# A four-layer graph kernel: layer norm's squares and result moved to ScalarE, biases as products of ones, hub sums by halving additions, and slack for some steps

## The chip, the cores and the metric

The kernel runs on one core of a Trainium2 chip. The metric is the time of one execution in microseconds of the device. A core has five engines, each with its own queue that it works through in order: PE (TensorE: matrix products and transposes), DVE (VectorE), ACT (ScalarE), POOL (GpSimd, which here issues the gathers and scatters by index) and SP (SyncE, which issues plain DMAs). They wait for each other only through semaphores.

## What is computed

The inputs are `x` (16 graphs of 1024 nodes with 64 features), a dense 0/1 adjacency matrix of 1024x1024 for each graph, a node mask and the weights of four layers. Each layer is a residual step, `x = layernorm(x + layer(x, adj))`:

```python
def _layernorm(x, axis=-1, eps=1e-5):
    m = jnp.mean(x, axis=axis, keepdims=True)
    v = jnp.var(x, axis=axis, keepdims=True)
    return (x - m) / jnp.sqrt(v + eps)
```

- Layers 0 and 3 take a weighted sum of three quantiles (0.25, 0.5, 0.75) over the values of each node's neighbours, per feature, after some neighbours have been removed by a rule on their rank (dilation). Then `h = relu((x + agg) @ W1 + b1)`, `y = (h @ W2 + b2) * mask`.
- Layer 1 is `adj @ (x @ weight) + bias`.
- Layer 2 is attention, `gelu((softmax(m1 m2^T) + adj) @ x @ GCN_W)`.

## The kernel before

The path that runs is `listed_path` (line 784). For each graph, `graph` (L964) makes lists of neighbours: `neighbours` (L994) finds the removed ones, `both_ways` and `order` rank the nodes by degree, and `lists` (L1102) turns all into indices and weights. The 128 nodes of highest degree are the hubs. Their long lists are cut into chunks of 32 slots, `CH`; two blocks of `HC` = 59 columns of chunks hold them. The other nodes form seven tiles of 128 nodes with 22 to 8 slots (`TILE_CAPS`).

A quantile layer is done 32 times (16 graphs, layers 0 and 3; the order is in `layers`, L1262, where layer 3 of a graph comes two graphs after its layer 0). For each one:

- `fetch_stream` (L1287) has POOL gather one row of features for each slot: 60 gathers for the hubs (`hrows`, a ring of eight groups of two) and 89 for the other tiles (`rows`). Between them it puts the nine scatters (`sums`) of the layer before.
- `turn_stream` (L1323) transposes the hub rows on PE (`turned`) into columns, which ACT copies out (`cols`). A group of four must be turned before POOL may go on in the ring. At the end it transposes the sums `tot`.
- `sort_stream` (L1377) sorts on DVE: the hubs' columns (`long_lists`, L1412), then the tiles (`rows`). Inside `long_lists`, `summed` (L1465) multiplies the sorted values by weights `hw` and adds them up into `tot`.
- `pick_stream` (L1391) scales the sorted `rows` by weights on ACT and adds them on PE (`picked`); ACT copies the result to `agg`, which POOL scatters into `sums`.
- `middle_stream` (L1639) reads `sums` back and does `last_step` (L1519): two small matrix products, bias, mask, residual and `layernorm` (L942). After layer 0 it goes on with `spread_layer` (L1561, layer 1) and `attention_layer` (L1572, layer 2), each with a layer norm at its end. That is 64 layer norms in all, each on a tile of 128 partitions with 8 x 64 values (`[P, NT, C]`).

All these are Python generators of steps. `give_out` (L211) merges them at build time into one order for each engine. It keeps a clock for each engine with estimated costs (`Queue.times`, L183), and gives out, again and again, the step with the earliest time `max(engine free, inputs ready + slack)`. `.after(n)` sets a step's slack to n ns: the step is ranked as if its inputs came that much later, so that steps of other streams go in front. The hardware then runs each engine's order as it stands. An instruction that waits holds all behind it on its engine. All steps are issued at line 180, so groups are told apart by their tiles.

Of the kernel before, what the change touches and what calls it, by code (L numbers as in the profile page):

```python
# [8 lines left out]
F32 = mybir.dt.float32  # L9
# [6 lines left out]
AF = mybir.ActivationFunctionType  # L16
ALU = mybir.AluOpType
AX = mybir.AxisListType
# [16 lines left out]
HC = 59  # L35
# [5 lines left out]
CH = 32  # L41
# [221 lines left out]
EPS = 1e-5  # L263
# [520 lines left out]
def listed_path(ctx: ExitStack, tc: tile.TileContext, x, adj, nodemask,  # L784
                l0_w1, l0_b1, l0_w2, l0_b2, l1_w, l1_b,
                l2_w1, l2_w2, l2_g, l3_w1, l3_b1, l3_w2, l3_b2, out, fp):
    nc = tc.nc
    B, N, C = x.shape
    H = l0_w1.shape[1]
    P = 128  # L790
# [90 lines left out]
    V.memset(w_scale[:, 0:1], 0.25)  # L881
    V.memset(w_scale[:, 1:2], 0.5)


    def load(ap, shape, name):
        t = const.tile(shape, F32, name=name)
        nc.sync.dma_start(t, ap)
        return t

    def rows(ap, name):  # L890
        t = const.tile([P, C], F32, name=name)
        nc.sync.dma_start(t, ap.rearrange("(o c) -> o c", o=1).to_broadcast([P, C]))
        return t

    ends = []
    for k, (w1, b1, w2, b2) in enumerate(((l0_w1, l0_b1, l0_w2, l0_b2), (l3_w1, l3_b1, l3_w2, l3_b2))):
        ends.append((load(w1, [C, H], f"w1_{k}"), load(b1.rearrange("(h o) -> h o", o=1), [H, 1], f"b1_{k}"),
                     load(w2, [H, C], f"w2_{k}"), rows(b2, f"b2_{k}")))
    l1w = load(l1_w, [C, C], "l1w")
    l1b = rows(l1_b, "l1b")  # L900

    l2g = const.tile([C + 1, C + 1], F32, name="l2g")
    V.memset(l2g, 0.0)
# [35 lines left out]
    def one(shape):  # L939
        return psm.tile(shape, F32, name="one", bufs=2)  # L940

    def layernorm(z, sq, y):  # L942
        s = small["t"].tile([P, NT], F32, name="ln_s")
        yield V.tensor_reduce(s, z, AX.X, ALU.add)
        mean = small["t"].tile([P, NT], F32, name="ln_mean")
        yield V.tensor_scalar(mean, s, 1.0 / C, None, ALU.mult)
        yield V.tensor_tensor(z, z, mean.unsqueeze(2).to_broadcast([P, NT, C]), ALU.subtract)
        yield V.tensor_mul(sq, z, z)
        v = small["t"].tile([P, NT], F32, name="ln_v")
        yield V.tensor_reduce(v, sq, AX.X, ALU.add)  # L950
        yield V.tensor_scalar(v, v, 1.0 / C, EPS, ALU.mult, ALU.add)
        r = small["t"].tile([P, NT], F32, name="ln_r")
        yield A.activation(r, v, AF.Sqrt)

        q = small["t"].tile([P, NT], F32, name="ln_q")
        yield V.reciprocal(q, r)
        yield V.tensor_mul(q, q, v)
        yield V.tensor_add(q, q, r)
        yield V.tensor_scalar(q, q, 0.5, None, ALU.mult)
        yield V.reciprocal(q, q)  # L960
        yield V.tensor_mul(y, z, q.unsqueeze(2).to_broadcast([P, NT, C]))
        return y

    def graph(b, k):  # L964
# [29 lines left out]
    def neighbours(np, psn, b, k, near, nbt):  # L994
# [24 lines left out]


        mi = small["g"].tile([P, NT], I32, name="mi")
        yield V.tensor_scalar(mi, pm, 1.0, None, ALU.add)
        do = small["g"].tile([P, NT], F32, name="do")
        yield V.scalar_tensor_tensor(do, pm, 10.0, k.mask, ALU.is_gt, ALU.mult)
        yield V.tensor_scalar(mi, mi, 1, None, ALU.logical_shift_right)
# [17 lines left out]
        for t in range(NT):  # L1043
            mine = slice(t * P, (t + 1) * P)
            v = np.tile([P, N], F16, name="v", tag="h", bufs=3)
            yield A.activation(v, pq.rearrange("p h n -> p (h n)"), AF.Abs, bias=mid[:, t:t + 1])
            gone = np.tile([P, N], F16, name="gone", tag="h", bufs=3)
            yield V.tensor_scalar(gone, v, off[:, t:t + 1], None, ALU.is_equal)
            if t + 1 < NT:
                pq = yield from counted(t + 1)  # L1050

            for h in range(NH):
                pn = psn.tile([P, HALF], F32, name="one")
                yield T.matmul(pn, neg16, gone[:, h * HALF:(h + 1) * HALF], start=True, stop=False)
                for j in range(HALF // P):
                    yield T.matmul(pn[:, j * P:(j + 1) * P], nbt[:, h * (HALF // P) + j, mine], ident16,
                                   start=False, stop=(j == HALF // P - 1))
                yield A.copy(near[:, t, h * HALF:(h + 1) * HALF], pn)
            pg = psn.tile([P, NT, P], F16, name="pg", tag="one")
            for j in range(NT):  # L1060
                yield T.transpose(pg[:, j, :], gone[:, j * P:(j + 1) * P], ident16)
            yield A.copy(nbt[:, :, mine], pg)
# [39 lines left out]
    def lists(lp, psl, b, near, perm, deg, k):  # L1102
# [46 lines left out]
        for q in range(GC):  # L1149
            yield T.matmul(pi, quarter[:, q], named.rearrange("s h (g q) -> s q h g", q=GC)[:, q],  # L1150
                           start=(q == 0), stop=(q == GC - 1))
        yield V.tensor_copy(k.hidx, pi)
        events.add(("hidx", b))


        for g in range(1, NT):
            pk = psl.tile([P, NH, HALF], F32, name="two")
            for h in range(NH):
                cols = slice(h * HALF, (h + 1) * HALF)
                yield T.matmul(pk[:, h], ones16[0:1, :], key_row[:, cols], start=True, stop=False)  # L1160
                for t in range(NT):
                    yield T.matmul(pk[:, h], perm[:, t, g * P:(g + 1) * P], near[:, t, cols],
                             start=False, stop=(t == NT - 1))
            cap = TILE_CAPS[g - 1]
            top = lp.tile([P, MOST + 2], F32, name="top", bufs=2)
            keys = pk.rearrange("p h n -> p (h n)")
            for r in range((cap + 7) // 8):
                yield V.max(out=top[:, 8 * r:8 * r + 8], in_=keys)
                if 8 * r + 8 < cap:
                    rest = lp.tile([P, N], F32, name="rest", bufs=2)  # L1170
                    yield V.match_replace(out=rest, in_to_replace=top[:, 8 * r:8 * r + 8], in_values=keys,
                                    imm_value=-4096.0)
                    keys = rest
            yield V.tensor_scalar(k.idx[:, g - 1, :cap], top[:, :cap], 0.0, None, ALU.max)
# [148 lines left out]
    def turn_stream():  # L1323
        for n, (l, b) in enumerate(layers):
# [3 lines left out]
            for g in range(0, NG, 4):  # L1328
                pt = psh.tile([P, 4 * P], F32, name="turned")
                for i in range(g, min(g + 4, NG)):  # L1330
                    yield Wait("h", n, i)
                    e = min(P, (2 * HC - i * GC) * CH)
                    yield T.transpose(pt[:, (i - g) * P:(i - g) * P + e], k.hrows[i][:e].rearrange("p h c -> p (h c)"),
                                      ident[:e, :e]).after(3000)
                events.add(("turned", n, g // 4))
                first, end = g * GC, min((g + 4) * GC, 2 * HC)
                for i in range(2):
# [74 lines left out]
    def long_lists(n, k):  # L1412
# [52 lines left out]
        def summed(block, spans):  # L1465

            yield Wait("hw", n, block)
            for c0, c1 in spans:
                assert len(set(side[c0:c1])) == 1
                v = bufs[side[c0]][block][:, :, c0 % HC:c0 % HC + c1 - c0]  # L1470
                yield V.tensor_tensor(v, v, k.hw[block][:, :, c0 % HC:c0 % HC + c1 - c0], ALU.mult)
            more = None
            for c0, first, lists, k0, chunks, by_list in HUB_RUNS:
                if c0 // HC == block:
                    v = bufs[side[c0]][block][:, :, c0 % HC:c0 % HC + lists * chunks]
                    v = v.rearrange("p s (l k) -> p l k s" if by_list else "p s (k l) -> p l k s", k=chunks)
                    if k0:
                        more = qp.tile([P, lists], F32, name="more")
                    yield V.tensor_reduce(more if k0 else k.tot[:, first:first + lists], v, AX.XY, ALU.add)
                    if k0:  # L1480
                        yield V.tensor_add(k.tot[:, first:first + lists], k.tot[:, first:first + lists], more)
            events.add(("block", n, block))

        yield from first(0)
# [34 lines left out]
    def last_step(n, l, b, k):  # L1519
# [6 lines left out]
        yield D.dma_start(ag, by_part(k.sums)).after(8000)  # L1526
        yield V.tensor_add(ag, ag, xn).after(5000)
        py = one([P, NT, C])
        for h in range(NH):
            ts = range(h * (HALF // P), (h + 1) * (HALF // P))  # L1530
            pt = one([C, HALF])
# [7 lines left out]
            yield A.activation(ht, ph, AF.Relu, bias=b1)  # L1539
            for t in ts:  # L1540
                c0 = t % (HALF // P) * P
                yield T.matmul(py[:, t, :], ht[:, c0:c0 + P], w2, start=True, stop=True)
        z = features("z")
        yield V.tensor_tensor(z, py, b2.unsqueeze(1).to_broadcast([P, NT, C]), ALU.add)
        yield V.tensor_mul(z, z, k.mask.unsqueeze(2).to_broadcast([P, NT, C]))
        yield V.tensor_add(z, z, xn)
        return (yield from layernorm(z, ag, features("y")))

    def by_adj(k, xn):
# [11 lines left out]
    def spread_layer(xn, k, y):  # L1561

        at_x = yield from by_adj(k, xn)
        po = one([P, NT, C])
        for t in range(NT):
            yield T.matmul(po[:, t, :], at_x[:, t * P:(t + 1) * P], l1w, start=True, stop=True)
        z = features("z")
        yield V.tensor_tensor(z, po, l1b.unsqueeze(1).to_broadcast([P, NT, C]), ALU.add)
        yield V.tensor_add(z, z, xn)
        return (yield from layernorm(z, features("ag"), y))  # L1570

    def attention_layer(xn, k, y):  # L1572
# [141 lines left out]
```

## Time and profile before

| | |
|---|---|
| Median of 3 runs | 8266.02 us (8259.21 to 8276.33) |
| The profiled execution, its own time | 8298.99 us |
| Its span in the trace | 8297.2 us |
| Mean granted TensorE clock in it | 0.738 |
| POOL: gathers and scatters | 5056 instructions, between 0.9 and 1.5 us each as a rule |
| First gather | 192.67 us after the span's start |
| ACT table loads | 50, 1283 ns each |

The span runs from the first to the last instruction. "Busy" time of an engine leaves out the time in which it issues or waits. The list of waits gives, for each pair of a waiting instruction and what released it, the total time, the number of times and the longest. A group of instructions is written as out<-in by the names of the tiles.

### The profile page before, as it was taken

Reading aid. Unit: us, or ns where it says so; the run is one execution under the profiler, and the core shown is the slowest. Engines: PE = TensorE matmul, PEld = TensorE weight load, DVE = VectorE, ACT = ScalarE, POOL = GpSimd, SP = SyncE. Lnnn points to the kernel's source line nnn. Section 1 sums busy time; section 2 is a strip of 40 time slices with the busy share of each in tenths; the row PEclk is TensorE's granted clock in tenths of the full one; section 3 lists DMA queues with packets and bytes.
Section 4 is the critical chain, followed back from the end, with each engine's and each line's share of the span. In section 5 each row is a group of like instructions: output and inputs, shape, how many; then the busy total and the mean of one; then the engine's idle time right before and its main releaser. Section 6 shows DMA issues by size and latency. Waiting matters only on the chain. (4 is left out here: it accounts for less than half of the span.)

```text
span 8297.2 us, 81388 instructions
## 1 busy us (share of the span) xinstructions
PE 5196.2 (63%) x24851; PEld 2751.4 (33%) x24851; DVE 7057.9 (85%) x14774; ACT 2329.8 (28%) x5554; POOL 5693.1 (69%) x5087
## 2 busy tenths in 40 slices
PE   6568777758475675856658575665856668272541
PEld 4244333333332333433233333323333233131221
DVE  2779798789898898988889898898988889979795
ACT  3324334142322324132242313324232232121121
POOL 0734677667776776767767676777767777777774
PEclk8778887878686776877778686777867678565565
DMA  1331423232323222232322324222332222232221
GB/s 48 72 72 50 99 44 97 46 77 65 73 50 89 52 55 69 62 81 52 63 63 66 73 50 94 52 51 69 72 71 52 65 61 65 33 68 33 58 42 22
DMA packets 762008, 513.78 MB, mean 62 GB/s; under 512 B 459098, under 2 KB 600538, under 8 KB 761306
## 3 DMA queue, kind: packets, MB, share of 16 engines
q1 hardware_dynamic: 457434, 261.99, 13.0%
q0 software_dynamic: 161792, 163.90, 11.6%
q10 hardware_dynamic: 142336, 82.59, 3.4%
q8 instruction: 201, 3.29, 0.2%
q14 instruction: 245, 2.01, 0.1%
HBM read 408.73 MB, written 103.55 MB: 62 GB/s over the span
## 5 line engine op out<-in xcount | busy, mean ns | idle before, releaser
L180 POOL DMA_INDIRECT rows<-table,idx x2848 | 3264.6, 1146 | 867.9 <-issue 841.1
L180 POOL DMA_INDIRECT hrows<-table,hidx x1920 | 2096.4, 1092 | 928.8 <-issue 443.1
L180 DVE TENSOR_TENSOR spare<-cols 128x528 f32<-128x528 f32 (+11 forms) x1632 | 1057.1, 674 | 71.4 <-ACT cols L180 47.7
L180 DVE TENSOR_TENSOR cols<-spare 128x528 f32<-128x528 f32 (+11 forms) x1664 | 1074.8, 680 | 15.8
L180 PE MATMUL picked<-rows,ident 128*128 128x64 f32 (+2 forms) x2496 | 646.1, 366 | 347.6 <-ACT rows L180 346.6
L180 PE MATMUL turned<-ident,hrows 128*128 128x128 f32 x960 | 343.1, 379 | 673.6 <-DMA hrows<-table,hidx 636.3
L180 POOL DMA_INDIRECT sums<-agg,node x224 | 260.2, 1162 | 665.2 <-DMA sums<-agg,node 195.3
L180 ACT ACTIVATE rows<-rows,wt 128x64 f32<-128x64 f32 x2272 | 612.5, 340 | 191.2 <-DVE rows L180 188.5
L180 PEld LDWEIGHTS picked<-rows,ident 128*128 128x128 f32 x2496 | 479.7, 244 | 543.1 <-ACT rows L180 446.3
L180 PE MATMUL pi<-hot,numbers 128*32 128x236 f16 x4096 | 549.4, 284 | 76.0 <-DVE hot L180 74.4
L180 DVE TENSOR_TENSOR spare<-rows 128x64 f32<-128x64 f32 (+8 forms) x1056 | 539.0, 541 | 58.1 <-DMA sums<-hagg,hnode 21.7
L180 PE MATMUL two<-near,perm 128*128 128x512 f16 x1792 | 544.6, 459 | 0.0
L180 PEld LDWEIGHTS <-numbers 128*32 128x32 f16 x4096 | 397.0, 103 | 331.8 <-issue 275.7
L180 ACT COPY cols<-turned 128x512 f32<-128x512 f32 (+3 forms) x288 | 148.5, 528 | 1253.8 <-PE turned L180 1252.9
L180 PE MATMUL two<-run,nbt 128*128 128x512 f16 (+3 forms) x1536 | 408.9, 438 | 142.4 <-ACT v L180 142.4
L180 PEld LDWEIGHTS turned<-ident,hrows 128*128 128x128 f32 x960 | 163.4, 175 | 926.5 <-issue 591.9
L180 PEld LDWEIGHTS <-nbt 128*128 128x128 f16 x3584 | 303.6, 113 | 491.4 <-issue 416.9
L180 DVE TENSOR_TENSOR rows<-spare 128x512 f32<-128x512 f32 (+9 forms) x896 | 462.5, 538 | 0.8
L180 PE MATMUL turned<-ident,tot 128*64 128x128 f32 x32 | 11.7, 365 | 609.4 <-DVE tot L180 609.4
L180 DVE TENSOR_TENSOR spare<-cols,spare 128x472 f32<-128x472 f32 (+2 forms) x704 | 379.2, 539 | 15.6
L180 PE MATMUL one<-xt,wt 64*128 64x512 f32 x512 | 369.8, 851 | 22.0 <-DVE top L180 22.0
L180 DVE TENSOR_TENSOR rows<-rows,spare 128x64 f32<-128x64 f32 (+4 forms) x1120 | 363.2, 329 | 17.6
(232 smaller groups left out, 10079.9 us busy)
## 6 DMA issues: line engine op xcount, KB each, us to landing
at<-adjt SPq DMA_DIRECT2D x512, 256.0 KB
a<-in_adj_dram SPq DMA_DIRECT2D x128, 512.0 KB
adjt<-at ACTq DMA_DIRECT2D x128, 512.0 KB
rows<-table,idx POOLq DMA_INDIRECT x2848
hrows<-table,hidx POOLq DMA_INDIRECT x1920
hw<-hwt SPq DMA_DIRECT2D x64, 472.0 KB
hwt<-ho ACTq DMA_DIRECT2D x64, 236.0 KB
ag<-sums SPq DMA_DIRECT2D x32, 256.0 KB
```

The source lines that it names most:

```text
L180: return Step(lambda: f(*args, **kw), self.engine, cost, late, reads, writes, "dma" in name)
```

## The change

- In `layernorm`, the subtraction of the mean, the product z*z and its sum over features leave DVE. ACT makes for each of the eight tiles of nodes a `Square` of z with the negative mean as bias, which also accumulates the sum. The result `y = z*q - mean*q` is made by eight ACT instructions with scale and bias in place of one DVE product; DVE gets a small product `mean*q`.
- In `last_step` and `spread_layer` the bias is no longer added on DVE. A matrix product of a row of ones with the bias row starts the accumulation in PSUM, and the others add to it. The bias is loaded as one row and not copied to 128 partitions. The mask is applied by eight scaled ACT copies out of PSUM; the residual is added on DVE.
- In `summed`, the weighted values go into one buffer, and the 32 slots are added by halves: 16, 8, 4, 2, 1. Then each run of lists needs one small operation on its chunks.
- Some steps get slack: `ln_v` 2000, the first `reciprocal` 1000, `mi` 3000, `gone` 2000, `hidx` 3000, the first `max` of each tile 1500, `z + xn` in `last_step` 6000 and `z` in `spread_layer` 3000; the transposes of the hub rows go from 3000 to 6000.

```diff
@@ layernorm
-        yield V.tensor_scalar(mean, s, 1.0 / C, None, ALU.mult)
-        yield V.tensor_tensor(z, z, mean.unsqueeze(2).to_broadcast([P, NT, C]), ALU.subtract)
-        yield V.tensor_mul(sq, z, z)
+        yield V.tensor_scalar(mean, s, -1.0 / C, None, ALU.mult)
         v = small["t"].tile([P, NT], F32, name="ln_v")
-        yield V.tensor_reduce(v, sq, AX.X, ALU.add)
-        yield V.tensor_scalar(v, v, 1.0 / C, EPS, ALU.mult, ALU.add)
+        for t in range(NT):
+            yield A.activation(sq[:, t], z[:, t], AF.Square, bias=mean[:, t:t + 1], accum_out=v[:, t:t + 1])
+        yield V.tensor_scalar(v, v, 1.0 / C, EPS, ALU.mult, ALU.add).after(2000)
...
-        yield V.reciprocal(q, r)
+        yield V.reciprocal(q, r).after(1000)
...
-        yield V.tensor_mul(y, z, q.unsqueeze(2).to_broadcast([P, NT, C]))
+        yield V.tensor_mul(mean, mean, q)
+        for t in range(NT):
+            yield A.activation(y[:, t], z[:, t], AF.Identity, scale=q[:, t:t + 1], bias=mean[:, t:t + 1])
@@ neighbours
-        yield V.tensor_scalar(mi, pm, 1.0, None, ALU.add)
+        yield V.tensor_scalar(mi, pm, 1.0, None, ALU.add).after(3000)
...
-            yield V.tensor_scalar(gone, v, off[:, t:t + 1], None, ALU.is_equal)
+            yield V.tensor_scalar(gone, v, off[:, t:t + 1], None, ALU.is_equal).after(2000)
@@ lists
-        yield V.tensor_copy(k.hidx, pi)
+        yield V.tensor_copy(k.hidx, pi).after(3000)
...
-                yield V.max(out=top[:, 8 * r:8 * r + 8], in_=keys)
+                yield V.max(out=top[:, 8 * r:8 * r + 8], in_=keys).after(0 if r else 1500)
@@ turn_stream
-                                      ident[:e, :e]).after(3000)
+                                      ident[:e, :e]).after(6000)
@@ summed
+            w = bufs[side[spans[0][0]]][block]
             for c0, c1 in spans:
                 assert len(set(side[c0:c1])) == 1
-                v = bufs[side[c0]][block][:, :, c0 % HC:c0 % HC + c1 - c0]
-                yield V.tensor_tensor(v, v, k.hw[block][:, :, c0 % HC:c0 % HC + c1 - c0], ALU.mult)
-            more = None
+                cols = slice(c0 % HC, c0 % HC + c1 - c0)
+                yield V.tensor_tensor(w[:, :, cols], bufs[side[c0]][block][:, :, cols], k.hw[block][:, :, cols], ALU.mult)
+            half = CH // 2
+            while half:
+                yield V.tensor_add(w[:, :half], w[:, :half], w[:, half:2 * half])
+                half //= 2
             for c0, first, lists, k0, chunks, by_list in HUB_RUNS:
                 if c0 // HC == block:
-                    v = bufs[side[c0]][block][:, :, c0 % HC:c0 % HC + lists * chunks]
-                    v = v.rearrange("p s (l k) -> p l k s" if by_list else "p s (k l) -> p l k s", k=chunks)
+                    v = w[:, 0, c0 % HC:c0 % HC + lists * chunks]
+                    v = v.rearrange("p (l k) -> p l k" if by_list else "p (k l) -> p l k", k=chunks)
+                    mine = k.tot[:, first:first + lists]
                     if k0:
-                        more = qp.tile([P, lists], F32, name="more")
-                    yield V.tensor_reduce(more if k0 else k.tot[:, first:first + lists], v, AX.XY, ALU.add)
-                    if k0:
-                        yield V.tensor_add(k.tot[:, first:first + lists], k.tot[:, first:first + lists], more)
+                        yield V.tensor_add(mine, mine, v[:, :, 0])
+                    elif chunks == 1:
+                        yield V.tensor_copy(mine, v[:, :, 0])
+                    elif chunks == 2:
+                        yield V.tensor_add(mine, v[:, :, 0], v[:, :, 1])
+                    else:
+                        yield V.tensor_reduce(mine, v, AX.X, ALU.add)
@@ last_step
         py = one([P, NT, C])
+        yield T.matmul(py, ones_row, b2.unsqueeze(1).to_broadcast([1, NT, C]), start=True, stop=False)
...
-                yield T.matmul(py[:, t, :], ht[:, c0:c0 + P], w2, start=True, stop=True)
+                yield T.matmul(py[:, t, :], ht[:, c0:c0 + P], w2, start=False, stop=(t == NT - 1))
         z = features("z")
-        yield V.tensor_tensor(z, py, b2.unsqueeze(1).to_broadcast([P, NT, C]), ALU.add)
-        yield V.tensor_mul(z, z, k.mask.unsqueeze(2).to_broadcast([P, NT, C]))
-        yield V.tensor_add(z, z, xn)
+        for t in range(NT):
+            yield A.activation(z[:, t], py[:, t], AF.Copy, scale=k.mask[:, t:t + 1])
+        yield V.tensor_add(z, z, xn).after(6000)
@@ spread_layer
         po = one([P, NT, C])
+        yield T.matmul(po, ones_row, l1b.unsqueeze(1).to_broadcast([1, NT, C]), start=True, stop=False)
         for t in range(NT):
-            yield T.matmul(po[:, t, :], at_x[:, t * P:(t + 1) * P], l1w, start=True, stop=True)
+            yield T.matmul(po[:, t, :], at_x[:, t * P:(t + 1) * P], l1w, start=False, stop=(t == NT - 1))
         z = features("z")
-        yield V.tensor_tensor(z, po, l1b.unsqueeze(1).to_broadcast([P, NT, C]), ALU.add)
-        yield V.tensor_add(z, z, xn)
+        yield V.tensor_tensor(z, po, xn, ALU.add).after(3000)
```

The rest of the diff makes the row of ones and loads the three biases as rows.

More of the change, by code (lines that the diff above doesn't have):

```diff
@@ L882, in listed_path @@
     V.memset(w_scale[:, 1:2], 0.5)
+    ones_row = const.tile([1, P], F32, name="ones_row")
+    V.memset(ones_row, 1.0)
     def load(ap, shape, name):
@@ L888, in load, with row @@
         return t
[L890 to L893, printed above, removed]
+    def row(ap, name):
+        return load(ap.rearrange("(o c) -> o c", o=1), [1, C], name)
     ends = []
@@ L897, in listed_path @@
         ends.append((load(w1, [C, H], f"w1_{k}"), load(b1.rearrange("(h o) -> h o", o=1), [H, 1], f"b1_{k}"),
-                     load(w2, [H, C], f"w2_{k}"), rows(b2, f"b2_{k}")))
+                     load(w2, [H, C], f"w2_{k}"), row(b2, f"b2_{k}")))
     l1w = load(l1_w, [C, C], "l1w")
-    l1b = rows(l1_b, "l1b")
+    l1b = row(l1_b, "l1b")
     l2g = const.tile([C + 1, C + 1], F32, name="l2g")
```

## The prediction

> **What bounds the kernel now.** I read the page first (busy shares, then the 40 slices), then the lists of POOL's and DVE's waits, then groups with their shapes, and last one stretch of the timeline.
>
> ```profile
> span 8297.2 us, 81388 instructions
> PE 5196.2 (63%) x24851; PEld 2751.4 (33%) x24851; DVE 7057.9 (85%) x14774; ACT 2329.8 (28%) x5554; POOL 5693.1 (69%) x5087
> POOL 0734677667776776767767676777767777777774
> L180 POOL DMA_INDIRECT rows<-table,idx x2848 | 3264.6, 1146 | 867.9 <-issue 841.1
> ```
>
> DVE leads with 85%, ACT has room. But POOL's 69% misleads: a gather takes 1.15 us, and then 0.30 us (868 us over 2848) pass in which it waits for nothing. A POOL that never waits still shows 7 tenths. What can be won there stands in the list of its waits (us in total, times, longest):
>
> ```profile
> POOL sums L180 <- DMA sums<-agg,node: 195.3, 109, 4.1
> POOL sums L180 <- ACT rows L180: 186.1, 34, 52.7
> POOL hrows L180 <- DVE hidx L180: 184.3, 1, 184.3
> POOL sums L180 <- ACT agg L180: 182.9, 19, 36.4
> POOL hrows L180 <- PE turned L180: 177.2, 99, 23.7
> ```
>
> The first is the scatters' own order and stays; the third is the start. ACT rows 186, ACT agg 183, PE turned 177 and the smaller ones (DVE rows, cols, spare, z, top and PE one: 89) make 635. Without them the span is 8297 - 635 = 7662, **POOL's floor**. In the steady part, 2000 to 7000 us, the same list gives 280: PE 112, ACT 109, DVE 59. DVE's own list:
>
> ```profile
> DVE gone L180 <- ACT v L180: 251.1, 105, 8.3
> DVE z L180 <- PE one L180: 227.5, 26, 18.2
> DVE top L180 <- PE two L180: 151.6, 57, 17.9
> DVE top L180 <- PE one L180: 56.4, 82, 2.2
> DVE hidx L180 <- PE pi L180: 53.2, 13, 6.5
> ```
>
> So two engines are near full. How one late engine holds the others shows at the end of one layer's hub work (start, duration, instruction, idle before it):
>
> ```profile
> 4096.16 1.23 DVE L180 TENSOR_REDUCE tot<-cols 128x20 f32<-128x640 f32 x1
> ...
> 4097.45 0.42 PE L180 MATMUL turned<-ident,tot 128*64 128x128 f32 x1 [37.73 <-DVE tot L180]
> ...
> 4098.97 1.45 POOL L180 DMA_INDIRECT hrows<-table,hidx  x1 [7.73 <-PE turned L180]
> ```
>
> DVE finished `tot` late; PE stood 37.7 us, and POOL, whose ring of hub rows was full, 7.7 us. DVE's instructions just ahead held a whole layer norm. This is why less DVE work should reach the end.
>
> **The change, part by part.** *Layer norm, 64 times.* Removed from DVE: `z<-z,ln_mean` 683 ns, `ag<-z` 682, `ln_v<-ag` 676, `y<-z,ln_q` 684, so 2.73 us; added: `mean*q`, like `ln_q<-ln_q,ln_v`, 0.16. Net 2.56 x 64 = 164 us. Added to ACT: 8 squares and 8 scalings of 128x64. The row for 128x64 with one column operand is `rows<-rows,wt`, 340 ns; an accumulated sum costs 220 to 241 more (the READ_ACCUMULATOR rows behind `near` and `v`). Squares: 8 x 0.57 = 4.6 us. Scalings have two column operands, which no row shows: at least the 214 of `agg<-picked` 128x64 without one, at most twice 340; nearest is 340, and I take that: 2.7. Together 7.3 x 64 = 467 us of ACT (bounds 400 to 640).
>
> *Biases and mask.* In `last_step` two DVE instructions go (692 + 683 ns, x32 = 44 us), and 8 scaled copies of 128x64 from PSUM come on ACT: 8 x 0.34 x 32 = 87 us. In `spread_layer` one of two goes: 0.68 x 16 = 11 us. PE gets 48 products of a row of ones, 512 columns wide; the nearest row is `one<-xt,wt` with 512 columns, 851 ns: 41 us, from nothing to that. They need no input of the layer and run ahead of the transposes, so PE's 37% idle time hides them; without that cover they cost the 41. The bias loads become smaller at the start; the start waits 184 us for the first lists, which hides that.
>
> *Hub sums, 32 times.* Removed, by shape: reductions of 2895, 632, 579, 415, 576, 794, 468 and 1232 ns and an addition of 165: 7.76 us. Added per block: additions of 944, 472, 236, 118 and 59 columns, by equal shapes 1150 + 650 + 404 + 281 + 214 = 2.70, twice; and eight small ones at 146 to 205 ns, 1.33 in all. 6.73 us, a gain of 1.03 x 32 = 33 us. But each halving waits for the one before, while independent instructions overlap: in the timeline the next starts some 0.08 us before the last ends. Ten links of 0.1 us eat 1.0 per layer. So this edit is worth 0 to 33; I take 16.
>
> DVE loses 164 + 44 + 11 + 16 = **235 us**.
>
> *Slack.* It moves a step to a later place among DVE's (or PE's) instructions; no instruction is added, and no DMA is among the moved ones. The steps it reaches on DVE wait 251 (`gone`) + 227 (`z`, whose sum now waits behind ACT's copies) + 152 (`top` from `two`) + 53 (`hidx`) + 27 (`mi`) + 15 (`ln_q`) = 726 us now, 422 of them in the steady part. The mean wait of `gone` is 2.4 us against a slack of 2; of `z` 8.7 against 6; of `hidx` 4.1 against 3. So I take half, 363. The wait of `z` for PE passes to ACT's copies: 227 us, behind which on ACT stand `v`, `cols` and `rows`; ACT's idle 72% covers it, and what it costs without that cover is rival (c). 122 of `top` and 103 of `gone` fall before 2000 us, where other work to put in front is scarce. New waits: `ln_v` now waits for eight squares on ACT, and behind it on DVE stand the sorts; cover is the slack of 2 us. At nothing to 4.6 us each it costs 0 to 294; I take 0.7, since ACT's `ln_r` held DVE only 15.3 us in 64. That is 45. So DVE's waits fall by 363 - 45, about 320.
>
> Doubling the transposes' slack to 6000 is two-sided: PE waits 636 us for `hrows` now, which should shrink; but the transposes free POOL's ring, eight groups or 22 us of gathers, and later ones can lengthen the 177.
>
> DVE's occupied time falls by 235 + 320 = 555. POOL can follow only as far as its 635, and what it wins is what counts. **Sum:** steady part: the waits released by DVE go (59); of PE's 112 two thirds (75), since the stretch above shows DVE behind them and the ring's slack speaks against all; of ACT's 109 half (54), as DVE comes sooner but ACT has more to do. 188. Outside it POOL waits for whole chains at the start; there I credit DVE's smaller work alone, 235 x 3297/8297 = 93. The tail is one serial chain: squares and scalings 7.3 + mask 2.7 for DVE's 2.56 + 1.37, so 6 longer. 188 + 93 - 6 = 275. The profiled execution takes 8299.0 by its own time (span 8297.2), the median of runs is 8266.0, 0.4% less. 8299 - 275 = 8024, by 0.996: **7992**, so 7990.
>
> One rule speaks against the change: the Trainium skill, ScalarE: Activation LUTs, section "Rules for kernel authors", wants multiply and add on VectorE, not ScalarE. The row agrees on the price: one 128x512 is 0.68 us on DVE, and 8 x 0.34 = 2.7 on ACT. Were the engine's own price what counts, layer norm and mask would add 554 - 208 = 346 us; but ACT is 28% busy and DVE 85%, so the page's rule does not decide here. The same page, section "What ACT_TABLE_LOAD costs", says that each pointer operand adds about 93 ns: an estimate from it for the scalings is 340 + 93 = 433 ns, which would make ACT's addition 515 instead of 467; no row shows it.
>
> **Rivals.**
> (a) *The slack gives nothing* (it does not do what it says): the waits move to the next step, as real lateness exceeds it. Then DVE gives 235 - 45 = 190, of which POOL follows about half, 95 to 130: 8135 to 8240, say 8170. For it: `gone`'s and `z`'s mean waits are above their slacks.
> (b) *DVE held nearly everything*: POOL's waits mostly go, 450 to 550 of 635: 7720 to 7820, say 7770. For it: the stretch above. Against: the scatters' waits at the start pass through ACT.
> (c) *Slower: ACT's queue.* Layer norm's 16 instructions stand in order on ACT, and wait for `ln_mean`, then for `q` on DVE (`ln_r` waits 247 us in 64 now, up to 36). Behind them are the scalings of `rows` and the copies of `agg`, for which POOL's scatters wait, and behind those all gathers. It decides from 275/64 = 4.3 us of extra POOL wait per layer norm. At 6 of its 7.3 us passed on: 384 - 275 = +109, 8375. For it: POOL's 369 us for ACT rows and agg. Against: ACT still ends near 36% busy (2330 + 554 of 8000), and only 109 of these lie in the steady part.
>
> **Chances.** Forecast, 7840 to 8130: 0.55. (a) 0.18. (b) 0.12, a little below it included. (c) 0.12. No change 0.03. The range leaves out (c), no change, and the outer part of (b), 0.05: 7750 to 8240. A measurement of this kernel tells about 0.2% from no change. Faster 0.85, same 0.03, slower 0.12.
>
> **What would show it.** DVE's busy time near 6820 us; ACT's near 2880 with squares near 340 ns and their accumulator reads near 220; `gone`, `z`, `top` and `hidx` with half their waits; POOL's waits for PE turned, ACT agg and ACT rows down from 546 to some 350. Wrong would be: POOL's waits for ACT grown; a gather that takes another time than 1.15 us (the floor moves: 0.1 us is 285 us over `rows`); new DVE waits for `ln_v` near 4 us; or PE turned grown by the ring.

## The result and the profile after

The kernel after takes 8255.0 us (median of 12 runs, 8217.05 to 8279.63); the kernel before on the same chip 8272.6 us (12 runs, 8258.16 to 8288.93). The ratio is 0.9974, with a 95% interval of 0.996 to 0.9988. So it is faster, clear of noise but only by a quarter of a percent: 17.6 us where some 275 were forecast, outside the range. The profiled execution has a span of 8258.9 us, 38 less than before's profiled one; half of that lies in the two executions picked, as the medians differ by 17.6 only. In two of the later batches, on two chips, every kernel took 13 to 17% longer, before 17%, with waits on PE, ACT and DVE that the profile puts to nothing in the program; the eight runs there are told as ratios alone, and six of those kernels were run again (labels ending in `_2`; "the first run" below is the one of these batches).

The page of after, its head, POOL's slices and the group of the gathers (busy, mean ns, idle time ahead):

```profile
span 8258.9 us, 83245 instructions
PE 5314.9 (64%) x24947; PEld 2777.2 (34%) x24947; DVE 6878.5 (83%) x14791; ACT 2726.7 (33%) x7346; POOL 5640.8 (68%) x5087
POOL 0635567657676776767777676777777777777774
L180 POOL DMA_INDIRECT rows<-table,idx x2848 | 3247.0, 1140 | 868.0 <-issue 840.3
```

DVE did lose work (7057.9 to 6878.5) and ACT gained it (2329.8 to 2726.7). POOL's slices, of 207 us each, have lost a tenth in the second, fifth, sixth, ninth and eleventh, and from the twelfth on in none: something is late in the first 2300 us that was not before. POOL's list of waits after:

```profile
POOL hrows L180 <- PE turned L180: 316.1, 110, 57.4
POOL hrows L180 <- DVE hidx L180: 180.3, 1, 180.3
POOL sums L180 <- DMA sums<-agg,node: 175.3, 99, 5.3
POOL sums L180 <- ACT rows L180: 150.2, 19, 45.7
POOL sums L180 <- ACT agg L180: 105.6, 5, 29.7
```

The waits for ACT fell from 369 to 256 us, but `PE turned` rose from 177 to 316. DVE's list:

```profile
DVE top L180 <- PE two L180: 161.9, 61, 6.7
DVE z L180 <- ACT z L180: 159.8, 27, 39.7
DVE deg L180 <- ACT near L180: 143.1, 12, 17.3
DVE gone L180 <- ACT v L180: 124.5, 77, 9.2
DVE top L180 <- PE one L180: 99.6, 80, 4.5
DVE ln_v L180 <- ACT ag L180: 66.1, 30, 3.8
...
DVE rs L180 <- PE one L180: 46.9, 26, 6.0
```

`gone` halved (251 to 125), `z` fell by 68, `hidx` from 53 to 7. In their place stand `top` (208 to 262 in its two rows), `ln_v`, and two that had hardly waited in before:

```profile
DVE deg L180 <- ACT near L180: 17.3, 1, 17.3
DVE rs L180 <- PE one L180: 1.9, 2, 1.7
```

All idle times of DVE over 0.1 us together went up, from 1069 to 1185 us.

**By stage.** The transposes of `tot`, one for each of the 32 quantile layers, cut the span into equal pieces of work (L0 to L31). Two layers make a pair, since the odd ones are shorter; the steady piece is L7 to L25, nine pairs. "POOL's own" is its gathers, the gaps of 0.3 us behind them and the scatters' own order; the rest of a pair are waits for other engines, with 1 to 3 us of gaps that the profile puts to nothing. Each figure comes from one execution, and the runs of after alone lie up to 63 us apart, so two or three us per pair tell nothing.

| us | L1 to L7 | one pair, L7 to L25 | POOL's own | POOL's waits | DVE busy / waits | L25 to L31 | after L31 |
|---|---|---|---|---|---|---|---|
| before | 1618.9 | 495.7 | 467.8 | 27.9 | 438.4 / 48.0 | 1322.1 | 160.4 |
| after | 1667.6 | 484.9 | 458.8 | 26.2 | 427.4 / 46.8 | 1325.8 | 168.8 |

Of the 38 us between the two spans, nine pairs bring 97; the layers 1 to 7 give 49 back, all from L25 on 12. And the pair's gain is not the one forecast: 9 of its 10.8 us are POOL's own time, not waits. About half of the 9 are shorter gathers and scatters (357.6 to 353.1 us busy per pair), the other half is the scatters' own order (18.4 to 13.7).

### The profile page after: what moved, and what is told of

Read it like the earlier page. It is cut to its first block, busy times and chain, and to the rows that moved or that the text cites. A ratio compares the mean times of both kernels' runs of the same rounds, so it can differ in the third digit from the quotient of the medians.

```text
span 8258.9 us, 83245 instructions
## 1 busy us (share of the span) xinstructions
PE 5314.9 (64%) x24947; PEld 2777.2 (34%) x24947; DVE 6878.5 (83%) x14791; ACT 2726.7 (33%) x7346; POOL 5640.8 (68%) x5087
## 3 DMA queue, kind: packets, MB, share of 16 engines
q1 hardware_dynamic: 457008, 261.89, 13.3%
## 5 line engine op out<-in xcount | busy, mean ns | idle before, releaser
L180 POOL DMA_INDIRECT hrows<-table,hidx x1920 | 2054.8, 1070 | 1069.3 <-issue 457.2
L180 PE MATMUL picked<-rows,ident 128*128 128x64 f32 (+2 forms) x2496 | 676.0, 388 | 399.8 <-ACT rows L180 398.9
L180 PEld LDWEIGHTS picked<-rows,ident 128*128 128x128 f32 x2496 | 500.8, 259 | 557.9 <-ACT rows L180 483.3
L180 PE MATMUL two<-run,nbt 128*128 128x512 f16 (+3 forms) x1536 | 426.4, 452 | 238.0 <-ACT v L180 238.0
L180 PE MATMUL pi<-hot,numbers 128*32 128x236 f16 x4096 | 521.1, 273 | 70.1 <-DVE hot L180 66.1
L180 PE MATMUL two<-near,perm 128*128 128x512 f16 x1792 | 507.0, 434 | 0.0
L180 DVE TENSOR_TENSOR spare<-spare 128x944 f32<-128x944 f32 (+11 forms) x672 | 451.2, 671 | 19.1
```

Source lines behind the costliest of these rows:

```text
L180: return Step(lambda: f(*args, **kw), self.engine, cost, late, reads, writes, "dma" in name)
```

## The experiments

The first theory was that POOL's own pace sets the steady time, so that DVE's saving has nothing to shorten there, and that the slacks only move waits about. The rivals were that ACT's longer layer norm takes the gain back, and that the doubled slack of the transposes does (where expectations use letters, P is the first theory, Q and R are these two rivals). All ratios are against before on the same chip.

| kernel | us | ratio (95%) | L1 to L7 | pair | POOL's own / waits | DVE busy / waits |
|---|---|---|---|---|---|---|
| no_slack | 8329.9 | 1.008 (1.0063 to 1.0098) | 1636.1 | 494.9 | 464.6 / 30.3 | 426.1 / 58.2 |
| slack_only | 8360.6 | 1.0109 (1.0094 to 1.0125) | 1637.1 | 498.3 | 464.6 / 33.7 | 439.0 / 49.9 |
| turned_3000 | 8272.1 | 0.9998 (0.9987 to 1.0009) | 1661.8 | 489.9 | 462.9 / 27.0 | 427.6 / 51.5 |
| ln_back_2 | 8327.8 | 1.0068 (1.0052 to 1.0085) | 1628.4 | 494.7 | 466.4 / 28.3 | 434.3 / 50.3 |
| deg_slack_2 | 8311.0 | 1.0035 (1.0023 to 1.0048) | 1676.1 | 490.1 | 467.9 / 22.2 | 425.1 / 54.6 |
| late_slack_2000_2 | 8214.9 | 0.9913 (0.9896 to 0.9929) | 1619.6 | 485.5 | 461.4 / 24.1 | 427.3 / 47.4 |
| pool_1480_2 | 8208.9 | 0.9916 (0.9902 to 0.9931) | 1634.7 | 482.6 | 468.1 / 14.5 | 427.2 / 44.7 |
| no_inside | 8094.4 | 0.9779 (0.9765 to 0.9793) | 1643.0 | 477.8 | 450.0 / 27.8 | 384.6 / 83.4 |
| half_hub_2 | 7894.3 | 0.9526 (0.9505 to 0.9547) | 1590.6 | 469.7 | 377.5 / 92.2 | 426.1 / 32.8 |
| half_both_2 | 7746.9 | 0.9348 (0.9329 to 0.9367) | 1542.5 | 467.5 | 372.2 / 95.3 | 384.6 / 72.9 |

After, no_slack, turned_3000, deg_slack_2, late_slack_2000_2 and pool_1480_2 hold the same instructions in six orders, and take from 8209 to 8330 us. So a difference of some tens of us between kernels with different instructions cannot be put to the instructions alone, the 17.6 us of the change included.

**no_slack**: the change's arithmetic without any new slack.

```diff
-        yield V.tensor_scalar(v, v, 1.0 / C, EPS, ALU.mult, ALU.add).after(2000)
+        yield V.tensor_scalar(v, v, 1.0 / C, EPS, ALU.mult, ALU.add)
...
-                                      ident[:e, :e]).after(6000)
+                                      ident[:e, :e]).after(3000)
```

> The changed kernel with every new slack taken back (the transposes of hub rows at 3000 again), its arithmetic kept. Theory P (in steady state POOL bounds and takes nearly the same time per pair of layers whatever DVE saves; what was gained there, some 105 us, is lost again at layers 2 and 5, where the new order lets POOL stand): the loss of 60 us at layers 2 and 5 goes, a pair of layers stays at 484 to 495 us, so 8140 to 8210 us. Rival Q (ACT's 400 us of new work and its new waits hold the copies behind them, and that eats the gain): ACT's work is the same, and DVE's waits come back, so 8250 to 8320. Rival R (the longer slack of the transposes lengthens POOL's ring wait, 177 to 316 us): the 140 us come back, near 8115.

8329.9 us, slower than before, though DVE's busy time per pair is 12 us lower. Its lists of POOL's and of DVE's waits have

```profile
POOL hrows L180 <- PE turned L180: 287.8, 101, 28.9
```

```profile
DVE gone L180 <- ACT v L180: 280.7, 97, 9.1
DVE z L180 <- ACT z L180: 244.5, 30, 32.9
```

DVE's saved time shows up again as DVE's waits (48.0 to 58.2 per pair), and POOL's did not shrink (30.3). So the change's arithmetic, which takes work from DVE, buys nothing in this order. The time is above what P (8140 to 8210) and Q (8250 to 8320) expected.

**slack_only**: before, with the same slacks on its own steps.

```diff
-            yield V.tensor_scalar(gone, v, off[:, t:t + 1], None, ALU.is_equal)
+            yield V.tensor_scalar(gone, v, off[:, t:t + 1], None, ALU.is_equal).after(2000)
```

> The kernel before with the slacks alone (on its own steps: z = py + b2 with 6000, the one in the spread layer with 3000, the rest as in the change, none on ln_v). P: the loss at the early layers comes without the arithmetic's gain; steady pairs at 485 to 495: 8270 to 8340 us. Q: DVE's waits go and ACT gets no work, so clearly faster, near 8150. R: POOL's ring waits grow as in the change, so slower by 100 or more, near 8370.

8360.6 us, slower too, above P's 8270 to 8340 and near R's 8370; the next run speaks against R. The slacks do not pay by themselves either. Arithmetic (+0.8%) and slacks (+1.1%) together give -0.26%: the effects do not add up. Each version is another order of all engines.

**turned_3000**: only the transposes' slack back to 3000.

> The changed kernel with the transposes of the hub rows at 3000 again, all else kept. R: POOL's waits for PE turned fall from 316 to some 180 us, time 8110 to 8150. P: the early loss stays, the ring matters little: within 25 us of the changed kernel. Q: no change of ACT's work: the same.

8272.1 us, 17 more than after (0.9998 against 0.9974): the doubled slack helps a little. The theory that it takes the gain away, which had 8110 to 8150 here, falls.

**ln_back**: the layer norm of before, all else as after.

```diff
-        for t in range(NT):
-            yield A.activation(sq[:, t], z[:, t], AF.Square, bias=mean[:, t:t + 1], accum_out=v[:, t:t + 1])
+        yield V.tensor_mul(sq, z, z)
...
+        yield V.tensor_reduce(v, sq, AX.X, ALU.add)
```

> The changed kernel with the layer norm of before (on DVE, without its slacks); biases, mask, hub sums and the other slacks as in the change. DVE gets 164 us back, ACT loses 453 us. Q (ACT's layer norm holds the copies and scalings behind it): faster than the change, 8150 to 8220. P (DVE's work is not what bounds): within 30 us of 8255. If DVE's work mattered as the prediction had it: 8255 + 100, 8340 or more.

> The change without layer norm's move to ACT, as in ln_back, on another chip. Q (ACT's new work eats the gain): 8150 to 8220. P (neither DVE's nor ACT's share of work is what bounds): within 30 us of 8255. DVE's work matters as predicted: 8340 or more.

The two runs differ in sign. The first gives 0.9834 (0.979 to 0.9878). The second gives 8327.8 us, 73 more than after: outside P's 30 us, and just under the 8340 of a DVE whose work counts. The theory of ACT's queue, which had 8150 to 8220, is not borne out by it. How much of the 73 us is layer norm's work is not shown, as orders of the same instructions differ by more.

**no_inside**: does DVE set the pace? Of the hubs' sort, four of the five passes inside the chunks are left out.

```diff
-            for j in (16, 8, 4, 2, 1):
+            for j in (1,):
```

> The changed kernel with four of the five passes of the hub sort inside chunks left out (only the pass of distance 1 is made), so that the hub values are not fully sorted; this takes some 730 us from DVE (per layer 8 instructions less for each of four widths: 2 x (988+705+804+372) x 4 ns) and nothing from POOL, PE or ACT. P: POOL's gathers remain, and a pair of layers cannot fall below some 467 us: 7850 to 8000 us. A theory that DVE still bounds: near 8255 - 730 x 0.85, about 7630. Q: ACT's and PE's waits for DVE shrink too, 7700 to 7800.

DVE's busy time falls by 42.8 us per pair, the pair by 7.1; DVE's waits rise from 46.8 to 83.4. What the pair did gain is POOL's own time (458.8 to 450.0), because the same gathers got shorter:

```profile
L180 POOL DMA_INDIRECT rows<-table,idx x2848 | 3144.3, 1104 | 868.0 <-issue 836.3
L180 POOL DMA_INDIRECT hrows<-table,hidx x1920 | 1988.5, 1036 | 1059.6 <-issue 461.1
```

1104 ns where after has 1140. So DVE does not set the pace of the steady part. The time, 8094.4 us, is above all that was expected; of the 160 us won, the nine pairs bring 64.

**half_hub**: does POOL? The second gather of each group of hub rows is left out.

```diff
-                for h in range(2):
-                    yield fetched(table, rows[:e, h, :], k.hidx[:e, h, g:g + 1])
+                yield fetched(table, rows[:e, 0, :], k.hidx[:e, 0, g:g + 1])
```

> The changed kernel with the second gather of every hub group left out (960 of POOL's 5056 gathers and scatters; the ring of hub rows is eight fixed tiles, their second half stays zero, so half of the hubs' sums are zero). DVE, ACT and PE keep all their instructions. P (POOL's own time sets the steady state: 459 of 485 us per pair of layers are gathers, gaps and the scatters' order): POOL needs 83 us less per pair and the time falls until DVE holds it, whose busy time and waits make 440 to 470 us: 7800 to 8050. Against P, a chain through DVE, PE and ACT bounds whatever POOL does: within 60 us of the changed kernel, 8195 to 8255.

> The second gather of every hub group left out, as in half_hub, on another chip (on the one before every kernel, the kernel before too, took 17% longer). P (POOL's own time sets the steady state): 7800 to 8050. A chain through DVE, PE and ACT that bounds whatever POOL does: 8195 to 8255.

0.9249 (0.9183 to 0.9315) in the first run, 7894.3 us in the second, in P's range. POOL's own time falls by 81 us per pair, the pair by 15, and POOL's waits grow from 26 to 92. Per us of relief that is no more than in no_inside (15 of 81, 7 of 43). What differs is POOL: in no_inside it waits hardly more than in after (27.8 for 26.2), here it waits for others in a fifth of the time. So POOL's own time is a limit, as P has it, but a second one stands 15 us behind it.

**half_both**: both together.

> half_hub_2 and no_inside in one: the second gather of every hub group left out (half of the hubs' sums are zero) and four of five passes of the sort inside chunks left out (values not fully sorted). Apart, they gave 361 and 160 us against the changed kernel. Two limits close to each other (POOL 459 us per pair, DVE with its chain about 465): each hides the other, so together more than the 521 of the sum, 7350 to 7650 us. One long chain through all engines: the gains add or less, 7730 to 7850.

> As half_both: second hub gathers and four of five passes of the hub sort left out together. Two limits close to each other: 7350 to 7650 us. One long chain: 7730 to 7850.

0.9236 (0.9176 to 0.9296) and 7746.9 us, near the 7730 to 7850 of one long chain. The pair is 467.5, hardly under half_hub's 469.7, though DVE is busy for 385 and POOL's own time is 372. POOL's list:

```profile
POOL hrows L180 <- PE turned L180: 991.5, 159, 65.3
```

So what holds the pair near 467 us is neither DVE's work nor POOL's own time. By the list it is a chain that passes through the hub rows and their transposes; that the written order fixes it is argued, not shown, and which of its links holds it (ring, transposes, the lists of the next graph) was not isolated.

**deg_slack**: the new wait of `deg` is given slack too.

```diff
-        yield V.tensor_tensor(deg, parts[:, :, 0], parts[:, :, 1], ALU.add)
+        yield V.tensor_tensor(deg, parts[:, :, 0], parts[:, :, 1], ALU.add).after(15000)
```

> The changed kernel with a slack of 15000 for the sum deg in both_ways, the step at which DVE now waits 143 us, 10 to 13 us in each pair of layers. S (this wait took the place of those that were removed: PE stands before a transpose whose gather has not landed, ACT's near waits for PE, DVE's deg for ACT, and DVE is then late for tot): that wait goes, the pair falls from 485 to 475, the time to 8080 to 8170. P in its strict form (POOL's own time bounds, 459 per pair, and the rest are waits that move elsewhere): 8210 to 8260. Q (ACT's new work): as P.

> Slack of 15000 for deg, as in deg_slack, on another chip. S (deg's wait took the place of those removed): 8080 to 8170, 0.978 to 0.988 of the kernel before. P in its strict form and Q: 8210 to 8260, 0.993 to 0.999.

0.9908 (0.9853 to 0.9963) in the first run; 8311.0 us in the second, 56 more than after and above both expectations. `deg` is back at 17 us in DVE's list, and others have taken the rest of its 143 us:

```profile
DVE z L180 <- ACT z L180: 246.4, 21, 45.8
...
DVE ln_v L180 <- ACT ag L180: 126.1, 37, 12.1
DVE slot L180 <- PE two L180: 103.4, 14, 13.4
DVE rank L180 <- ACT v L180: 74.8, 13, 11.5
```

`z` 160 to 246, `ln_v` 66 to 126, `slot` 26 to 103, `rank` 12 to 75. This is how a wait moves rather than goes.

**late_slack_2000**: the slacks act only once the merge's clock of POOL has passed 2000 us; before that all slacks are those of before.

```diff
         free[h.engine] = t + h.cost
+        Queue.late = free.get("G", 0.0) > 2000000
...
-        yield V.reciprocal(q, r).after(1000)
+        yield V.reciprocal(q, r).after(1000 if Queue.late else 0)
```

> The changed kernel, in which the new slacks count only once POOL's clock in the merge has passed 2000 us (before that the old values hold). Theory E (the slacks' order in the first layers loses what the steady state gains; there, layers 2 and 5 are 35 and 27 us longer than before): the stretch from layer 1 to layer 7 falls from 1668 to about 1630 us, pairs stay at 485, 8205 to 8230 us. Against E, the early loss belongs to the arithmetic: 8245 to 8275.

> As late_slack_2000: the new slacks count only after 2000 us of POOL's clock in the merge. E (the early loss is the slacks' order): layers 1 to 7 take about 1630 us in place of 1668, pairs stay near 485, 8205 to 8230 us. Against E: 8245 to 8275.

0.9847 (0.9776 to 0.9918) in the first run; 8214.9 us in the second, as theory E had it. L1 to L7 is 1619.6 us, as in before (1618.9), the pair stays at 485.5. So, as a sum, the 49 us lost there come from the slacks acting early. POOL's list (its line is 181, as the file has a line more above it):

```profile
POOL hrows L181 <- PE turned L181: 241.2, 120, 28.8
```

75 us less than after's 316.1, and the wait of 57.4 is gone.

**pool_1480**: the merge reckons each of POOL's gathers and scatters at 1480 ns for 1420. A pair has 316 of them (two layers of 60 + 89 + 9), and POOL's own time over 316 is 1480 ns in before (467.8) and 1452 in after (458.8), the scatters' own order included.

```diff
-            return (1420, 3000) if name == "indirect_dma_start" else (1000, 200)
+            return (1480, 3000) if name == "indirect_dma_start" else (1000, 200)
```

> The changed kernel with the order made for a slower POOL: the cost that the merge reckons for a gather or scatter is 1480 ns in place of 1420 (the trace has 459 us for 316 of them in a pair, 1452 each, with the scatters' order). Nothing else changes but the order. S: steps behind a gather are put later, PE waits less than its 663 us for hrows, and DVE and POOL wait less: pair 470 to 478, time 8120 to 8200. P: POOL's time is the same, 8230 to 8270. Q: the same.

> The order made with 1480 ns for a gather in place of 1420, as in pool_1480, on another chip. S: 8120 to 8200, PE's waits for hrows well below 663. P and Q: 8230 to 8270.

0.9896 (0.9844 to 0.9947) and 8208.9 us. The time lies between what the two theories expected (8120 to 8200 and 8230 to 8270). No instruction is different; the merge only has a longer time for POOL to go by, and orders the others for it. POOL's waits per pair fall from 26.2 to 14.5, but its own time goes back from 458.8 to 468.1, as in before, so that the pair is only 2.3 us shorter; L1 to L7 is 33 us shorter. Two lines of POOL's list:

```profile
POOL hrows L180 <- PE turned L180: 211.6, 118, 29.6
POOL sums L180 <- DMA sums<-agg,node: 206.2, 108, 5.1
```

Both this and late_slack_2000 beat both kernels: their intervals lie wholly below after's 0.996.

**hub_back, bias_back**: the hub sums, or the biases and the mask, as before.

> The changed kernel with the hub sums of before (reductions in place of halvings); DVE gets some 33 us back by the rows, 1 us per layer just ahead of tot, for which PE waits. If the DVE work ahead of tot sets when POOL's ring goes on: 8270 to 8300. If POOL's own time bounds: within 15 us of 8255.

> The changed kernel with biases and mask on DVE as before (slack 6000 and 3000 on the first step of each); DVE gets 55 us back, ACT loses 60 and PE 48 products. DVE's wait for ACT's copies of z (160 us) becomes a wait for PE. If less DVE work is what the change gains from: 8275 to 8320. If POOL's own time bounds: within 20 us of 8255.

1.0464 (1.0399 to 1.0529) and 1.0003 (0.9946 to 1.0059), both only in those batches. Beside after's 0.9974 they would say that both parts help, but other kernels' ratios there were up to 0.028 from those of their second runs (half_hub 0.9249 and 0.9526). hub_back is 0.049 above after, more than that and far above what was expected; it was not run again. So the shares of these two parts stay open.

## Why the prediction was wrong, step by step

**The costs on DVE and ACT** were about right. The times of DVE's instructions, added up, fell by 237 us (7849 to 7612) where 235 were forecast. But neighbours overlap, by 791 us in before and 734 in after, so busy time fell by 179 only. The price on ACT was in the bounds. The groups of ACT after, with their shapes:

```profile
L180 ACT ACTIVATE ag<-z,ln_mean 128x64 f32<-128x64 f32 x512 | 171.1, 337 | 219.4 <-DVE ln_mean L180 219.0 <-DVE hd L180 0.4
L180 ACT ACTIVATE y<-z,ln_mean,ln_q 128x64 f32<-128x64 f32 x384 | 136.0, 427 | 93.5 <-DVE ln_mean L180 93.3
L180 ACT ACTIVATION_READ_ACCUMULATOR ag<-z,ln_mean 128x1 f32 x512 | 96.9, 189 | 0.0
L180 ACT ACTIVATE z<-one,mask 128x64 f32<-128x64 f32 x256 | 59.7, 331 | 35.6 <-PE one L180 35.6
```

Squares 337 (340 taken), accumulator reads 189 (220), mask copies 331 (340), scalings with two column operands 427 ns (340 taken). With the 128 scalings into `x` that is some 573 us by rows (554 forecast), yet busy time rose only by 397: the reads lie mostly inside the next square (171.1 and 96.9 us cover 186 together), and scalings and mask copies run into their neighbours (384 of 427 ns would be 164 us, and cover 136.0). The Trainium skill, ScalarE: Activation LUTs, section "What ACT_TABLE_LOAD costs", has 93 ns for each pointer operand; put on the 340 ns of the row, that is an estimate of 433 for the scalings, and 427 agrees. The products of ones cost 76 us of PE (57.7 + 17.9 in their groups) for 41 forecast, which took each for one instruction; they are 96 in the trace, two for each product. They wait for nothing.

**DVE's waits fall by about 320.** This failed. The named ones fell as forecast or nearly (`gone` -127 of 126 expected, `hidx` -47, `mi` -18, `z` -68 of 114), but `top`, of which 76 were to go, rose by 54, `ln_v` came with 66 (45 forecast), and the total rose by 116. Why they come back is seen in one place in the steady part (the timeline of after; the brackets give the idle time before and what ended it):

```profile
4339.11 0.42 PE L180 MATMUL turned<-ident,tot 128*64 128x128 f32 x1 [6.54 <-DVE tot L180]
...
4344.99 0.94 POOL L180 DMA_INDIRECT hrows<-table,hidx  x1 [0.31 <-issue]
...
4348.71 0.45 PE L180 MATMUL turned<-ident,hrows 128*128 128x128 f32 x1 [9.18 <-DMA hrows<-table,hidx]
...
4351.44 0.45 PE L180 MATMUL turned<-ident,hrows 128*128 128x128 f32 x1 [2.29 <-DMA hrows<-table,hidx]
...
4355.34 0.60 ACT L180 ACTIVATE near<-one 128x512 f16<-128x512 f32 x1 [15.52 <-PE one L180]
...
4361.13 0.17 DVE L180 TENSOR_TENSOR deg<-parts 128x8 f32<-128x8 f32 x1 [13.26 <-ACT near L180]
```

PE's order has the transposes of the next hub rows after that of `tot`. POOL, never idle for more than 0.3 us, reaches these rows only at 4345, so PE stands 9 us; a product stands behind the transposes, ACT's `near` waits 15.5 us for it and DVE's `deg` 13.3 us for ACT. DVE's wait is POOL's lateness, passed on. A faster DVE waits longer (no_inside: 83 us per pair for 47), and a slack on `deg` only picks who waits, as deg_slack_2 showed.

**Steady part, -188 of POOL's waits.** This is the step that failed most. Forecast: of 280 us between 2000 and 7000, 188 go when DVE is relieved. Measured: 27.9 to 26.2 per pair, which is 17 us in those ten pairs. ACT's part did go (10.5 to 1.5 per pair), but `PE turned` took more than half of it (8.5 to 14.3) and POOL's waits for DVE rose (6.5 to 8.4). What the steady part gained all the same, 10.8 per pair or some 109 us, is nearly all POOL's own time, which the forecast held fixed: that part of the 188 came by luck and not by the mechanism. It is no firm property of the new arithmetic either, as the same instructions in the orders of pool_1480_2 and deg_slack_2 have 468 us of it again. The error lay before the fractions: that waits of a pacing engine end when their named releaser gets less work. POOL's own 468 of 496 us in before left under 6% to win, and the orders of the same work share these waits out differently: 22 to 30 us per pair in no_slack, turned_3000, deg_slack_2 and late_slack_2000_2, 14.5 in pool_1480_2.

**Outside it, -93.** It failed in sign: L1 to L7 +49, L25 to L31 +4. The prediction looked at the stretch before 2000 us only as one where "other work to put in front is scarce". In fact the new order put too much in front. The timeline of after in layer 5:

```profile
1679.56 1.06 PE L180 MATMUL turned<-ident,hrows 128*128 128x128 f32 x4
...
1680.25 0.94 POOL L180 DMA_INDIRECT hrows<-table,hidx  x1 [57.44 <-PE turned L180]
```

POOL stood 57.4 us, since PE's order had attention's products and the next graph's lists ahead of these four transposes. Layers 2 and 5 (from L1 to L2 and from L4 to L5) are the ones that grew: 335.3 to 369.8 and 286.9 to 314.1 us. With late_slack_2000_2 the loss of L1 to L7 goes as a sum, but these two are still 355.1 and 295.8 us, much as in no_slack (355.6 and 293.1): about half of their growth comes with the new arithmetic's order and not with the slacks. The merge's own clock already had the two 18.5 and 39 us longer than in before, and it starts its last step at 7886.9 us in after, 7885.7 in before and 7828.4 in late_slack_2000_2. So it saw no gain in the change and 58 us in the later slacks; it could be read without a chip.

**The end, +6** came as +8.4: right.

**The rivals.** (c), ACT's queue, is refuted: POOL's waits for ACT fell, and ln_back_2 is slower, though by no more than orders differ. (a) had the mechanism, waits that pass to the next step, but not its price: the slacks are worth 75 us beside this arithmetic (8329.9 to 8255.0), and alone they cost 1.1%. It also let POOL follow half of DVE's saving, where it followed little. (b) is refuted by no_inside: relieving DVE nearly four times as much as the change does gives 7 us per pair and 8094 us in all, far from 7770. The sign of "`PE turned` grown by the ring", named as what would make the prediction wrong, is what came, but not by the doubled slack, since turned_3000 is slower.

## What to carry to other kernels

Before a saving on one engine is counted, split the period of the engine that paces the kernel into its own work, its fixed gaps and its waits. As long as its own work takes the same time, only the waits can be won, and here, with queues in a fixed order, most of them passed to another instruction instead of ending. Ask of every result whether the order alone could have made it: six orders of the same instructions spread over 121 us here, seven times the change's gain. Judge slack or cost constants of a planner by the whole order that they make, stage by stage and at the start apart from the steady part; here a higher cost of the pacing engine's instructions in the planner and a later start of the slacks were each worth more than the whole change.

## What was not expected of the hardware

A gather's time depends on what DVE does beside it. In after, the 410 gathers in whose first 0.94 us no DVE instruction runs take 944 ns on average; the 2691 that have only TENSOR_TENSOR beside them take 1153; the 60 beside only MAX8 and TENSOR_REDUCE take 947. In before it is 945 (405 gathers), 1174 (2575), and 945 beside TENSOR_REDUCE alone (82). Not every one is longer: 37% of the 2691 took at most 960 ns, like the one at 4343.74. The timeline of after, with DVE at work, mostly TENSOR_TENSOR, until 4347.9 and idle from there to 4361.1:

```profile
4340.29 1.42 POOL L180 DMA_INDIRECT rows<-table,idx  x1 [0.30 <-issue]
4342.02 1.42 POOL L180 DMA_INDIRECT rows<-table,idx  x1 [0.30 <-issue]
4343.74 0.94 POOL L180 DMA_INDIRECT rows<-table,idx  x1 [0.30 <-issue]
...
4350.23 0.94 POOL L180 DMA_INDIRECT hrows<-table,hidx  x1 [0.30 <-issue]
4351.48 0.94 POOL L180 DMA_INDIRECT hrows<-table,hidx  x1 [0.30 <-issue]
4352.73 0.94 POOL L180 DMA_INDIRECT hrows<-table,hidx  x1 [0.30 <-issue]
```

This fits no_inside, where DVE spends 12% less time in TENSOR_TENSOR (5061 us for 5762) and the gathers are 34 to 36 ns shorter. It does not explain why they are also shorter in after than in before, where TENSOR_TENSOR takes less (5717 us). The Trainium skill, SBUF — State Buffer, section "Who interferes with whom", says that a DVE instruction with two SBUF inputs contends with a GpSimd instruction that reads SBUF; from a probe in which `tensor_tensor` did not stall a DMA it infers that the making of descriptors needs another interface than the one `tensor_tensor` takes. These rows agree with the first, as a gather takes its indices from SBUF (`idx`, `hidx`); whether they bear on the second, no run here tells. So the two engines that the prediction treated as apart were not: at 4768 gathers, the distance from 1153 to 944 ns gives an estimate of 0.2 us each that goes with the kind of DVE's instructions beside them.
